# One decoder layer on Trainium2: projections whose PSUM bank is read once, and tasks that run before the weighted values

## The chip, the cores and the metric

The kernel runs on one core of a Trainium2 chip. A core has five engines with queues of their own: PE (matmul; its weight loads are listed as PEld), DVE (vector), ACT (scalar, activations), POOL and SP, which here only issues DMAs. Matmuls write to PSUM, which has eight banks of 128 partitions x 2 KB; DVE and ACT read it. An engine works its instructions in the order in which the program lists them and waits where an operand isn't ready. The metric is the device time in microseconds (us), the median over runs.

## The reference

A decoder layer on x of 4 x 1024 x 256 (batch, sequence, features), 16 heads of 16 features, everything in f32:

```python
x = x + self_attn(layernorm(x), w_qkv, w_out)             # windows of 128
x = x + cross_attn(layernorm(x), ctx, mask, Wq, bq, ...)  # 77 keys of context
x = x + ffn(layernorm(x), ...)                            # SwiGLU, int8 fake-quantised
```

Self-attention cuts the sequence into chunks of 128. The queries of a chunk see the keys of their own chunk, causally, and of the chunk before (the first chunk has none before). Scores are divided by sqrt(16), then softmax, then the weighted sum of the values, then `w_out`. Cross-attention has biases on q, k and v, 77 keys per batch entry, and a mask over these keys; in this data all rows of the mask are the same. The feed-forward part scales x, weights and hidden values to int8 steps and back. The change touches the two attention stages; of the rest only the queues of some transfers.

## The kernel before

**Heads and strips.** The 256 features are two halves (g). In a half, 128 features on 128 partitions are eight heads of 16 rows. They are handled as four strips (j) of 32 partitions; each strip holds an even and an odd head (o = 0, 1). A matmul on a strip contracts over its 32 rows. For head o the tile of the queries, `q[g, o]`, and of the keys, `k[g, o]`, therefore has the 16 rows of the *other* head emptied, and one of these spare rows does a service: in `k` it holds ones, and in `q` the negated maximum of each query's scores, so that the matmul of the weights yields score minus maximum. In cross-attention a second spare row of `q`, the next one, holds ones, and the keys' tile has the mask there; the first spare row is zero until the maximum arrives.

**Making q and k** (`project`, L344). 16 matmuls (L304) fill one bank, `ps_p`, with the projection of 512 columns (half a sequence, `hf`) for a half g. Then ACT reads the bank twice, once for each o, and multiplies by a column of ones and zeros per partition: L363 for queries in cross-attention (`qrows` carries the scale of the scores, the bias column the row of ones), L367 for queries and L369 for keys in self-attention. 48 projections run in the loop and its lead: 32 for self-attention, 16 for cross-attention.

**A unit of attention.** Work goes in units: of self-attention two query tiles for one (g, o), of cross-attention four, 96 in all, one *slot* each. Four steps belong to a unit or a group of units:

- `maxima` (L714): PE computes the scores of four strips into four banks `sc_n`, with queries on partitions (L725 for self-, L740 for cross-attention); DVE takes the maxima of each strip (L755: two instructions per strip with the causal mask; L766: one per strip).
- `put_maxima` (L774): once per (g, o) PE transposes the maxima (`ps_mx`, L777), ACT copies them to `mxT` (L781), and four DMAs on SP (L784) put them into the spare row of each strip of `q`.
- `weights` (L799): the scores again, keys on partitions, into four banks `sc_t` (L810, L839), whose order is that of the strips; ACT takes the exponential (L820, L842), and POOL zeroes what causality excludes (L824).
- `weighted_values` (L845): PE sums the values by the weights into one bank `ps_av` (L854, L864); DVE transposes it to `o_sb` (L878). `normalise` (L880) divides by the sum of the weights on DVE (`rec` L886, `aN` L888), and `by_features` (L895), for odd o only, transposes both heads' results to `aT` (L900).

**The order of the work** is written out by the loop at L1214. The maxima run five slots (`LEAD`) ahead of the weights. A slot does, in this order: the weighted values that are due, with normalise and by_features; *tasks* from a list with a cost, an earliest slot and a due slot (projections, `values`, the layer norm's transposes `ps_t`, `out_project` into `ps_op`, preparation of weights), up to 1.35 of cost; *asides* for DVE (layer-norm statistics at L192 and L194, quantising of weights at L598 to L608, up to 1.2); `put_maxima` where due; the maxima of a unit ahead; the weights of the present unit. The last slots (`tail`) have an order of their own. All these groups draw on one pool of eight banks that goes round: a group takes the oldest bank, and waits until its readers are done.

**Queues.** SP issues the loads, the maxima's transfers and most stores; ACT issues the last two stores at the end of the feed-forward part (L1522).

Of the kernel before, what the change touches and what calls it, by code (L numbers as in the profile page):

```python
# [18 lines left out]
P = 128  # L19
# [6 lines left out]
def decoder_layer(  # L26
# [175 lines left out]
    with ExitStack() as att:  # L202
# [14 lines left out]
        rows, qrows, onerow, nextrow = [], [], [], []  # L217
        for o in range(NS):
            m = wp.tile([P, 1], F32, name=f"rows{o}")
            w = wp.tile([P, 1], F32, name=f"onerow{o}")  # L220
            n2 = wp.tile([P, 1], F32, name=f"nextrow{o}")
            for dst, first, n in (
                (m, o * HD, HD),
                (w, (1 - o) * HD, 1),
                (n2, (1 - o) * HD + 1, 1),
            ):
                at = stage.tile([P, NJ, HD], F32, name="at", tag="at", bufs=4)
                nc.gpsimd.memset(at, 0.0)
                nc.gpsimd.affine_select(
                    out=at[:, :, 0:n],  # L230
                    in_=at[:, :, 0:n],
                    compare_op=ALU.not_equal,
                    fill=1.0,
                    base=-first,
                    pattern=[[-SL, NJ], [-1, n]],
                    channel_multiplier=1,
                )
                nc.vector.tensor_reduce(dst, at, AX.XY, ALU.max)
            q = wp.tile([P, 1], F32, name=f"qrows{o}")
            nc.vector.tensor_scalar(q, m, QSCALE, None, ALU.mult)  # L240
            rows.append(m)
            qrows.append(q)
            onerow.append(w)
            nextrow.append(n2)


        f = stage.tile([P, P], F32, name="cb_f", tag="stage")
# [96 lines left out]
        def project(job, g, which, hf):  # L344

            out = job.q if which == "q" else job.k
            w = job.wq if job.kind == "X" else (wq_s if which == "q" else wk_s)
            if hf == 0:
                for o in range(NS):
                    out[g, o] = next_of("qk", qks)  # L350
            ps = bank("ps_p")
            for c in range(NC):
                by_columns(
                    ps,
                    w[:, c, g * P : (g + 1) * P],
                    job.xnT[hf][:, c, :],
                    start=(c == 0),
                    stop=(c == NC - 1),
                )
            for o in range(NS):  # L360
                dst = out[g, o][:, hf * HS : (hf + 1) * HS]
                if job.kind == "X":
                    nc.scalar.activation(  # L363
                        dst, ps, AF.Identity, bias=job.bq[:, g, o : o + 1], scale=qrows[o]
                    )
                elif which == "q":
                    nc.scalar.activation(dst, ps, AF.Copy, scale=qrows[o])  # L367
                else:
                    nc.scalar.activation(dst, ps, AF.Identity, bias=onerow[o], scale=rows[o])  # L369
# [39 lines left out]
        begin.close()  # L409

        def attention(alike):
            turn.update(begun)
            arm = ExitStack()
# [14 lines left out]
            bq_p = wp.tile([P, NP, NS], F32, name="bq_p")  # L428
# [8 lines left out]
            def prep_cross():  # L437
# [4 lines left out]
                def load_biases():  # L442
                    with nc.allow_non_contiguous_dma(reason="256-element biases"):
                        for name, src in (("q", bq), ("k", bk)):
                            raws[name] = small.tile([P, NP], F32, name="raw_b")
                            nc.sync.dma_start(out=raws[name], in_=src.rearrange("(g p) -> p g", p=P))
                    nc.sync.dma_start(out=bv_b, in_=bv.partition_broadcast(SK))
                    nc.sync.dma_start(out=bo_b, in_=bo.partition_broadcast(P))

                def biases():  # L450
                    for name, dst, by, plus in (("q", bq_p, qrows, nextrow), ("k", bk_p, rows, onerow)):
                        for o in range(NS):
                            nc.vector.tensor_scalar(dst[:, :, o], raws[name], by[o], None, ALU.mult)
                            nc.vector.tensor_scalar(
                                dst[:, :, o], dst[:, :, o], plus[o], None, ALU.add
                            )

                def transposed(w, name, dst=None):
                    def load():
                        raws[name] = stage.tile([P, NC, D], F32, name="raw_w", tag="stage")  # L460
                        nc.sync.dma_start(out=raws[name], in_=w.rearrange("(c p) i -> p c i", p=P))
# [17 lines left out]
                def load_context():  # L479
                    raws["c"] = stage.tile([SK, B, D], F32, name="craw", tag="stage")  # L480
                    nc.sync.dma_start(out=raws["c"], in_=ctx_in.rearrange("b k d -> k b d"))
# [55 lines left out]
                def load_row():  # L537
                    raws["m"] = stage.tile([P, SK], I32, name="mrow", tag="stage")
                    nc.sync.dma_start(out=raws["m"], in_=mask[0, :].partition_broadcast(P))

                def add_row():
# [7 lines left out]
                    for o in range(NS):  # L549
                        for g in range(NP):  # L550
                            at = (1 - o) * HD + 1
                            nc.sync.dma_start(
# [4 lines left out]
                def load_mask():  # L557
                    raws["m"] = stage.tile([P, NT, SK], I32, name="mraw", tag="stage")
                    nc.sync.dma_start(out=raws["m"], in_=mask.rearrange("(t p) k -> p t k", p=P))
# [50 lines left out]
            def prep_ffn():  # L610


                def rows_of(w, dst, sc, f):
                    kept = {}

                    def load():
                        kept["raw"] = stage.tile([P, D], F32, name="raw_f", tag="stage")
                        if f < NF - 1:
                            nc.sync.dma_start(out=kept["raw"], in_=w[f * P : (f + 1) * P, :])
                        else:  # L620
                            for r in (0, HR):
                                nc.sync.dma_start(out=kept["raw"][r : r + HR], in_=w[f * P :, :])
# [18 lines left out]
                def down(c):  # L641
                    kept = {}

                    def load():
                        kept["raw"] = stage.tile([P, FF], F32, name="raw_d", tag="stage")
                        nc.sync.dma_start(out=kept["raw"], in_=w_down[c * P : (c + 1) * P, :])
# [127 lines left out]
            def put_maxima(job, g, o):  # L774
# [6 lines left out]
                nc.scalar.copy(mxT, ps[: NJ * NT, :P])  # L781
                for j in range(NJ):
                    row = j * SL + (1 - o) * HD
                    nc.sync.dma_start(  # L784
# [338 lines left out]
            for j, job in enumerate(jobs):  # L1123
# [59 lines left out]
                if S_:  # L1183
                    for t2 in range(NT // 2):
                        a, by = ((-3, -1) if j else (-1, -1), (-1, 1), (3, 3), (4, 4))[t2]
# [28 lines left out]
            for slot in range(first, last):  # L1214
# [21 lines left out]
                else:  # L1236
                    for args in values_of.get(slot, ()):
                        weighted_values(*args)
                        normalise(*args, tail)
                        if not tail:  # L1240
                            by_features(*args)
                spent = 0.0
                cap = 1.35 if now and ahead else 2.3
                while t := next_in(tasks, slot, spent, cap):
# [3 lines left out]
                    if fn is out_project:  # L1248
                        job, hf, t2 = args
                        if job.kind == "X" and t2 == HT // 2 - 1:  # L1250
                            third_norm(job.b, hf, slot)
                spent = 0.0
# [27 lines left out]
        def feed_forward():  # L1280
# [155 lines left out]
            for t0 in sorted(added_there):  # L1436
                nc.sync.dma_start(out=rows_out(t0), in_=xb[t0 // NT][:, t0 % NT : t0 % NT + 2, :])
# [59 lines left out]
            def down(q, t0, nt):  # L1497
                odd = t0 // HT % 2
                for t2 in range(nt // 2):
# [20 lines left out]
                    else:  # L1520
                        nc.vector.tensor_tensor(y, y, xb[b][:, t : t + 2, :], ALU.add)
                        (nc.scalar if t0 + 2 * t2 >= B * NT - 4 else nc.sync).dma_start(  # L1522
                            out=rows_out(t0 + 2 * t2), in_=y
                        )
# [70 lines left out]
```

## Time and profile before

| | us |
|---|---|
| median of 3 runs | 665.53 (665.24 to 666.23) |
| profiled execution, its own time | 663.93 |
| its span on the chip | 662.1 |
| PE busy, with waits inside a group | 613.3 (93%) |
| DVE busy | 542.7 (82%) |
| ACT busy | 367.6 (56%) |
| POOL busy | 268.8 (41%) |

The span is the time from the first to the last instruction; 1.8 us of the execution's own time lie around it. TensorE's granted clock was 0.99 of full speed. A row of the timeline gives the start, the time, the engine, the line and operation, the tile written and those read, and how many instructions it stands for; in brackets is the idle time before it and what ended that. Ends of matmuls are modelled, so the time of a group on PE is best read from its start to the start of the next. A row of the waits gives engine, line, the releaser, the sum of the waits, how often, and the longest. "who waited for it" counts the waits of other instructions that this line ended.

In 40 equal slices of the span, PE's and DVE's busy shares in tenths are these; the two attention stages fill about slices 2 to 32:

```profile
PE   9899999999999999999999999999999997787775
DVE  6878778868779799678997996897978787889896
```

### The profile page before, as it was taken

What the parts mean: (1) busy time and instruction counts of PE and PEld (TensorE: products, weight loads), DVE (VectorE), ACT (ScalarE), POOL (GpSimd) and SP (SyncE); (2) the same over time, 40 slices, a digit from 0 to 9 for tenths busy, and PEclk for the clock granted to TensorE, in tenths of its full rate; (3) what the DMA queues carried; (4) which work ended last, traced back from release to release, by engine and by line L of the source; (5) the groups of instructions that cost most, each with busy time, mean ns of one, the idle gap of its engine ahead of it and who ended that gap; (6) DMA issues with size and microseconds to landing.
All of it is one profiled execution on the core that took longest, in us unless ns stands there. A gap on an engine that the chain in (4) does not pass through costs nothing.

```text
span 662.1 us, 20220 instructions
## 1 busy us (share of the span) xinstructions
PE 613.3 (93%) x7857; PEld 350.9 (53%) x7862; DVE 542.7 (82%) x1922; ACT 367.6 (56%) x672; POOL 268.8 (41%) x520
## 2 busy tenths in 40 slices
PE   9899999999999999999999999999999997787775
PEld 6456566566555665654446666544443445333564
DVE  6878778868779799678997996897978787889896
ACT  2365564644555634645565366447556475788392
POOL 3164533647234667650044867526611141111032
PEclk9999999999999999999999999999999999989899
DMA  8100100000000000000000000000000020000057
GB/s 291 48 4 15 38 3 2 18 5 5 18 27 10 12 2 19 9 15 14 8 10 11 12 24 26 5 3 4 3 2 4 4 96 17 1 0 1 0 97 165
DMA packets 18080, 17.43 MB, mean 26 GB/s; under 512 B 2998, under 2 KB 17335, under 8 KB 17975
## 3 DMA queue, kind: packets, MB, share of 16 engines
q1 hardware_dynamic: 15239, 13.69, 6.4%
q0 software_dynamic: 1904, 1.84, 2.1%
q8 instruction: 64, 1.05, 0.7%
q10 hardware_dynamic: 832, 0.53, 0.3%
q14 instruction: 41, 0.34, 0.2%
HBM read 9.47 MB, written 6.03 MB: 23 GB/s over the span
## 4 chain that ended last, share of the span: by engine, by line
PE 61%; DVE 25%; ACT 7%; issue 5%; POOL 1%; DVEq 0%; ACTq 0%
PE ps_p L304 13%; PE ps_av L854 8%; PE sc_t L810 7%; PE sc_n L725 7%; PE ps_op L304 6%; PE ps_av L864 4%; PE sc_t L839 3%; DVE junk L755 3%; PE ps_v L304 3%; PE sc_n L740 3%; DVE bnst L192 2%; DVE o_sb L878 2%; ACT shared L369 2%; PE ps_idle L117 2%; DVE aT L900 2%
## 5 line engine op out<-in xcount | busy, mean ns | idle before, releaser
L755 DVE CUSTOM_DVE_ANT_0 junk<-sc_n,cboth 128x256 bf16<-128x256 f32 (+1 forms) x512 | 172.3, 402 | 35.1 <-PE sc_n L725 35.1
L820 ACT ACTIVATE pt<-sc_t 128x512 f32<-128x512 f32 (+1 forms) x256 | 125.4, 577 | 85.3 <-PE sc_t L810 85.3
L824 POOL TENSOR_SCALAR_AFFINE_SELECT pt<-pt 128x256 f32<-128x256 f32 x256 | 102.2, 407 | 116.1 <-ACT pt L820 105.5
L810 PE MATMUL sc_t<-shared 32*128 32x256 f32 (+1 forms) x1024 | 87.9, 377 | 1.4 <-DVE vx L530 0.3
L842 ACT ACTIVATE ptx<-sc_t 77x512 f32<-77x512 f32 x128 | 65.2, 596 | 37.0 <-PE sc_t L839 37.0
L725 PE MATMUL sc_n<-shared 32*128 32x256 f32 (+1 forms) x1024 | 73.6, 387 | 3.0 <-ACT shared L369 1.6
L810 PEld LDWEIGHTS sc_t<-shared 32*128 32x128 f32 x1024 | 65.5, 185 | 13.6 <-ACT shared L367 3.2
L320 POOL TENSOR_SCALAR xn<-x,mv,rs 128x256 f32<-128x256 f32 x56 | 69.6, 1249 | 0.0
L160 POOL TENSOR_SCALAR ve<-mv 128x4 f32<-128x4 f32 x20 | 4.6, 232 | 153.8 <-DVE mv L194 153.7
L878 DVE STREAM_TRANSPOSE o_sb<-ps_av 128x512 f32<-128x512 f32 x63 | 45.0, 714 | 24.4 <-PE ps_av L854 14.3
L304 PE MATMUL ps_p<-shared,w_s 128*32 128x512 f32 x512 | 60.9, 595 | 3.4 <-DVE mx L766 1.6
L725 PEld LDWEIGHTS sc_n<-shared 32*128 32x128 f32 x1024 | 45.7, 184 | 32.3 <-DVE mx L755 10.8
L854 PE MATMUL ps_av<-pt,vt 128*32 128x256 f32 (+1 forms) x1152 | 59.3, 349 | 3.0 <-DVE mx L755 2.6
L766 DVE TENSOR_REDUCE mx<-sc_n 128x4 f32<-128x308 f32 x128 | 51.8, 466 | 8.5 <-PE sc_n L740 8.3
L854 PEld LDWEIGHTS ps_av<-pt,vt 128*32 128x32 f32 x1152 | 34.9, 110 | 31.5 <-DVE mx L755 6.4
L839 PE MATMUL sc_t<-shared,kx 32*77 32x512 f32 x256 | 45.9, 599 | 0.0
L755 DVE DVE_READ_ACCUMULATOR2_ANT mx<- 128x1 f32 x512 | 42.4, 83 | 0.1
L864 PE MATMUL ps_av<-ptx,vx 77*32 77x512 f32 x256 | 35.9, 605 | 3.4 <-DVE mx L766 2.5
L363 ACT ACTIVATE shared<-ps_p,bq_p,qrows 128x512 f32<-128x512 f32 x32 | 23.1, 773 | 26.0 <-PE ps_p L304 26.0
L740 PEld LDWEIGHTS sc_n<-kx,shared 32*128 32x128 f32 x1024 | 31.7, 186 | 10.2 <-DVE rec L886 1.7
L740 PE MATMUL sc_n<-kx,shared 32*128 32x77 f32 x1024 | 36.5, 277 | 0.0
L1406 ACT ACTIVATE act<-pg,gsc 128x512 f32<-128x512 f32 x44 | 29.2, 687 | 11.4 <-PE pg L1391 6.3
(201 smaller groups left out, 984.8 us busy)
## 6 DMA issues: line engine op xcount, KB each, us to landing
x<-in_x_dram SPq DMA_DIRECT2D x8, 512.0 KB
shared<-mxT SPq DMA_DIRECT2D x128, 4.0 KB
out_dram<-x SPq DMA_DIRECT2D x7, 256.0 KB
out_dram<-shared POOLq DMA_DIRECT2D x7, 256.0 KB, 4.6
out_dram<-shared SPq DMA_DIRECT2D x7, 256.0 KB
w_s<-in_L_attn_w_qkv_dram SPq DMA_DIRECT2D x2, 384.0 KB
raw_d<-in_L_ffn_w_down_dram SPq DMA_DIRECT2D x2, 352.0 KB
raw_f<-in_L_ffn_w_gate_dram SPq DMA_DIRECT2D x5, 128.0 KB
```

The source lines that it names most:

```text
L304: nc.tensor.matmul(out[r], lhsT[:, r], rhs, skip_group_check=True, **on)
L320: eng.tensor_scalar(xn, xb[job.b][:, t, :], job.st[hf].mv[:, i, 0:1], job.st[hf].rs[:, i : i + 1], ALU.subtract, ALU.mult,)
L725: nc.tensor.matmul(banks[j][:, (i + 1) * 2 * P - n : (i + 1) * 2 * P], q[r, t * P : (t + 1) * P], k[r, k0 * P : k0 * P + n], start=True, s ...
L740: nc.tensor.matmul(banks[j][:, i * SK : (i + 1) * SK], q[r, t * P : (t + 1) * P], k[r, :], start=alike, stop=alike or i == HT - 1,)
L755: nc.vector.tensor_tensor_reduce(out=junk[:, 2 * P - n :], in0=banks[j][:, (i + 1) * 2 * P - n : (i + 1) * 2 * P], in1=cboth[:, 2 * P - n ...
L810: nc.tensor.matmul(banks[j][:, w : w + n], k[r, t * P : (t + 1) * P], q[r, t * P : t * P + n], start=True, stop=True,)
L820: nc.scalar.activation(pt.rearrange("p i a q -> p (i a q)")[:, :w], banks[j][:, :w], AF.Exp)
L824: nc.gpsimd.affine_select(out=pt[:, :, 0, :], in_=pt[:, :, 0, :], compare_op=ALU.is_ge, fill=0.0, base=0, pattern=[[0, 2], [1, P]], channe ...
L839: nc.tensor.matmul(banks[j][:SK], k[r, :], q[r, s], start=alike, stop=True)
L842: nc.scalar.activation(pt, banks[j][:SK], AF.Exp)
L854: nc.tensor.matmul(ps[j * SL : (j + 1) * SL, (a0 - t0) * P : (a1 - t0) * P], slot_of(job.vs[kb // 2][:, kb % 2], heads[j]), job.pts[g, o, ...
L864: nc.tensor.matmul(ps[j * SL : (j + 1) * SL, :], slot_of(vx[:, job.b], heads[j]), job.pts[g, o, j, hf], start=True, stop=True,)
```

## The change

It has four parts.

1. `project` reads `ps_p` once. The first ACT instruction takes the whole bank, both heads' rows, to one head's tile in SBUF (q: o = 1, k: o = 0, cross-attention: o = 1, with the bias and the scale); nothing is masked there. The second instruction copies that tile, from SBUF, to the other head's tile, with the column of ones and zeros as its scale. In the unmasked tile the other head's rows are harmless only where the other operand is zero, so which tile may stay unmasked is alternated between q and k.
2. The rows of ones (and, in cross-attention, of zeros) come by transfers from small constant tiles, `none_one` (rows of zeros or ones, filled by POOL at the start): in self-attention one transfer per (g, o), in `put_maxima`, ahead of those of the maxima, into the spare rows of `k`; in cross-attention two per projection, zeros into row 0 and ones into row 1 of each strip of `q[g, 1]`. That is 16 and 32 transfers, all on SP for this data. `qrows` and most of the small DVE work on biases go.
3. In the loop, tasks come ahead of the weighted values, normalise and by_features, except in the tail. The window of the second quarter of the values' projections starts one slot later, (0, 1) instead of (-1, 1).
4. Transfers go by a name, `queue_of[0]`: SP where the mask's rows are all the same, as here, ACT otherwise. With it the last two stores move from ACT's queue to SP's.

```diff
-            for o in range(NS):
-                dst = out[g, o][:, hf * HS : (hf + 1) * HS]
-                if job.kind == "X":
-                    nc.scalar.activation(
-                        dst, ps, AF.Identity, bias=job.bq[:, g, o : o + 1], scale=qrows[o]
+            half = [out[g, o][:, hf * HS : (hf + 1) * HS] for o in range(NS)]
+            if job.kind == "X":
+                nc.scalar.activation(
+                    half[1], ps, AF.Identity, bias=job.bq[:, g : g + 1], scale=QSCALE
+                )
+                nc.scalar.activation(
+                    half[0], half[1], AF.Identity, bias=nextrow[0], scale=rows[0]
+                )
+                for row in range(2):
+                    queue_of[0].dma_start(
+                        out=half[1][row : P : SL, :].rearrange("j (t q) -> j t q", q=P),
+                        in_=none_one[row].unsqueeze(1).to_broadcast([NJ, HT, P]),
                     )
-                elif which == "q":
-                    nc.scalar.activation(dst, ps, AF.Copy, scale=qrows[o])
-                else:
-                    nc.scalar.activation(dst, ps, AF.Identity, bias=onerow[o], scale=rows[o])
+                return
+            first = 1 if which == "q" else 0
+            nc.scalar.activation(half[first], ps, AF.Copy, scale=QSCALE if which == "q" else 1.0)
+            nc.scalar.activation(half[1 - first], half[first], AF.Copy, scale=rows[1 - first])
...
                 nc.scalar.copy(mxT, ps[: NJ * NT, :P])
+                if job.kind == "S":
+                    queue_of[0].dma_start(
+                        out=job.k[g, o][(1 - o) * HD : P : SL, :].rearrange(
+                            "j (t q) -> j t q", q=P
+                        ),
+                        in_=none_one[1].unsqueeze(1).to_broadcast([NJ, NT, P]),
+                    )
                 for j in range(NJ):
                     row = j * SL + (1 - o) * HD
-                    nc.sync.dma_start(
+                    queue_of[0].dma_start(
...
-                        a, by = ((-3, -1) if j else (-1, -1), (-1, 1), (3, 3), (4, 4))[t2]
+                        a, by = ((-3, -1) if j else (-1, -1), (0, 1), (3, 3), (4, 4))[t2]
...
-                else:
+                elif tail:
                     for args in values_of.get(slot, ()):
                         weighted_values(*args)
                         normalise(*args, tail)
-                        if not tail:
-                            by_features(*args)
                 spent = 0.0
                 cap = 1.35 if now and ahead else 2.3
                 while t := next_in(tasks, slot, spent, cap):
...
+                if not tail:
+                    for args in values_of.get(slot, ()):
+                        weighted_values(*args)
+                        normalise(*args, tail)
+                        by_features(*args)
                 spent = 0.0
                 while t := next_in(beside, slot, spent, 1.2):
...
-                        (nc.scalar if t0 + 2 * t2 >= B * NT - 4 else nc.sync).dma_start(
-                            out=rows_out(t0 + 2 * t2), in_=y
-                        )
+                        queue_of[0].dma_start(out=rows_out(t0 + 2 * t2), in_=y)
```

## The prediction

> **What bounds the kernel now.** I read five views of the one profiled execution, in this order: the busy times with the chain that ended last, the groups by line, who waited for the reads of the projections' bank, the timeline of some slots, and SP's waits. A change within 0.2% (1.3 us) is about what a measurement of this kernel cannot tell from none.
>
> ```profile
> PE 613.3 (93%) x7857; PEld 350.9 (53%) x7862; DVE 542.7 (82%) x1922; ACT 367.6 (56%) x672; POOL 268.8 (41%) x520
> PE 61%; DVE 25%; ACT 7%; issue 5%; POOL 1%; DVEq 0%; ACTq 0%
> L755 DVE CUSTOM_DVE_ANT_0 junk<-sc_n,cboth 128x256 bf16<-128x256 f32 (+1 forms) x512 | 172.3, 402 | 35.1 <-PE sc_n L725 35.1
> ```
>
> PE looks full, but its 93% holds waiting: a matmul group that waits for a bank of PSUM in its middle counts as busy. DVE carries 25% of the chain, so the loop between PE and DVE is as much of a bound as PE itself. ACT, with 56%, matters only where PE waits for one of its results. Next, who waited for ACT's three reads of ps_p:
>
> ```profile
> L363 ACT ACTIVATE shared<-ps_p,bq_p,qrows x32: 768/772/780, 256.4 to 500.7; 128x512 f32<-128x512 f32 x32
> ...
>   PEld sc_t L839: 3.1, 7
>   PEld sc_t L810: 2.5, 7
> ...
> L367 ACT ACTIVATE shared<-ps_p,qrows x32: 679/684/689, 14.1 to 345.7; 128x512 f32<-128x512 f32 x32
> ...
>   PEld sc_t L810: 3.2, 10
> ...
> L369 ACT ACTIVATE shared<-ps_p,onerow,rows x32: 767/774/779, 15.8 to 351.7; 128x512 f32<-128x512 f32 x32
> ...
>   PEld sc_t L810: 2.9, 6
> ```
>
> Weight loads of the weights' scores (sc_t) wait for the second of the two reads: its last bank is the one that the projection left. The timeline of a slot with weighted values and a projection (207.7 to 214.0; rows of other engines left out) shows the price and DVE's part:
>
> ```profile
> 206.17 1.61 PE L810 MATMUL sc_t<-shared 32*128 32x256 f32 x16
> 207.71 1.94 PE L854 MATMUL ps_av<-pt,vt 128*32 128x128 f32 x40
> 209.47 1.90 PE L304 MATMUL ps_p<-shared,w_s 128*32 128x512 f32 x16
> 211.29 1.15 PE L725 MATMUL sc_n<-shared 32*128 32x256 f32 x16
> 212.26 1.82 PE L810 MATMUL sc_t<-shared 32*128 32x256 f32 x16
> 214.01 1.92 PE L304 MATMUL ps_p<-shared,w_s 128*32 128x512 f32 x16
> ```
> ```profile
> 209.72 0.72 DVE L878 STREAM_TRANSPOSE o_sb<-ps_av 128x512 f32<-128x512 f32 x1 [0.51 <-PE ps_av L854]
> 210.47 0.25 DVE L886 RECIPROCAL rec<-o_sb 128x16 f32<-128x16 f32 x1
> 210.75 0.42 DVE L888 TENSOR_TENSOR aN<-o_sb,rec 128x256 f32<-128x256 f32 x1
> 211.21 0.71 DVE L900 STREAM_TRANSPOSE aT<-aN 128x512 f32<-128x512 f32 x1
> ...
> 212.53 0.41 DVE L755 CUSTOM_DVE_ANT_0 junk<-sc_n,cboth 128x256 bf16<-128x256 f32 x1
> ```
>
> From start to next start, the projection is 1.82 us, ps_av 1.76, sc_n 0.97, and sc_t 1.75; where nothing waits (192.83) sc_t takes 1.04. DVE does its chain (o_sb, rec, aN, on odd heads aT) while PE does the projection, then 0.68 us of asides, then the maxima. That cover is what the new order takes away.
>
> **Part 1: one read of the bank.** Removed: one of two reads of ps_p in 48 projections. The bank comes free some 0.7 us sooner (pair 1.45 us as in the row at 185.72, one alone at most 0.77). The slot at 185.55 needed it 1.17 us after the projection's end: two reads miss that, one read does not. In 15 slots with a projection and without weighted values (14 of self-attention, 1 of cross-attention) sc_t now lies 0.59 us over its free length on average: -8.8 us. In slots with weighted values I count the same gain with part 3. The waits shown sum to 11.7 us of weight loads; matmuls lose more, since the loads are refilled after the wait. So -8.8 is between 0 (if another wait ends last there) and -15 us.
>
> The second copy now waits on the first, on ACT's own queue; behind it stand mxT's copy and the exponentials. ACT's idle before the exponentials is 85.3 us on sc_t alone, so a few tenths there are covered; without cover 64 pairs x 0.1 us = 6 us at most. A source in SBUF costs no more by the rows: L939, two pointer operands, 256 columns, 514 ns; the PSUM reads with two pointers, 512 columns, 773 ns.
>
> [...]
>
> **Part 2: spare rows by transfers.** Added: 48 transfers on SP. Sixteen stand before the four of mxT in SP's queue:
>
> ```profile
> SPq L784 <- ACT mxT L781: 369.5, 32, 19.1
> ```
>
> SP idles there, and the new transfer waits only for PE's last use of k and for ACT, both a slot earlier, so it should be issued in that idle time: 0. Without that cover: one issue of 0.7 us (four take 2.80 at 202.16) delays the last row, which lands 3.54 us after the first issue with 0.47 us to spare: 16 x 0.23 = 3.7 us; at worst a landing (1.37 us) is added, 16 x 1.6 = 26 us. The 32 of cross-attention go ahead three slots early, 1.4 us of SP per projection, and cover is ample: 0, at most 16 x 0.2 = 3 us. The last two output transfers on SP instead of ACT: one more issue (0.7 us) at most behind another, 0; the two memsets on POOL and some seven small DVE instructions fewer lie in the start: 0 to -1 us.
>
> [...]
>
> **Part 3: tasks ahead of the weighted values.** In some 53 slots of attention both exist (30 self-, 23 cross-attention). New order: task (1.84 us), ps_av, sc_n, sc_t on PE; on DVE the chain can begin only when ps_av ends. During the task DVE finishes the maxima of the slot before and then idles, 1.5 us, which no other work fills: its queue holds o_sb next. The next slot's first group takes over the bank of sc_n's first strip (the pool of eight goes round, four sc_n and four sc_t to a slot), so PE waits until DVE has read it. From ps_av's end: 0.2 + chain 1.47 (2.21 with aT) + asides + first strip 0.75, against sc_n + sc_t = 2.01 us. That leaves 0.41 us (1.15 with aT) of waiting, plus the asides; in cross-attention, whose first strip takes 0.5 us and whose two groups 1.92, it is 0.24 (0.98).
>
> - By durations: 16 x 0.41 + 14 x 1.15 + 12 x 0.24 + 11 x 0.98 = 36.4 us, and 33 us of asides in these slots (0.6 to 1.2 us in 39 of them, counted to 1.0): 69 us.
> - By three slots of the trace that have this order already, because they have no task:
>
> ```profile
> 70.70 0.85 PE L810 MATMUL sc_t<-shared 32*128 32x256 f32 x16
> ...
> 71.36 0.71 DVE L900 STREAM_TRANSPOSE aT<-aN 128x512 f32<-128x512 f32 x1
> ...
> 72.66 1.92 PE L304 MATMUL ps_p<-shared,w_s 128*32 128x512 f32 x16 [1.11 <-DVE mx L755]
> ```
>
> Here sc_t takes 1.96 us instead of 0.89: 1.07 lost with aT and no asides. At 285.61, with 0.88 us of asides, PE waits till 288.10, 1.6 lost; at 507.60 in cross-attention 1.3 (mean 1.45 with both); at 503.73, with neither, 0. So 20 slots with aT and asides x 1.45, 5 with aT only x 1.07, 19 with asides only x 0.71 (1.45 less aT's 0.74), 9 with neither x 0.2: 50 us.
>
> From this comes off what the same 53 slots lose now, 25.7 us, their waits for the second read (14 us) among it. Part 3 costs +24 by stretches, +43 by durations; with part 1's -8.8, +15 or +35. I take +22, nearer the stretches, which are the order itself, though few. 663.9 (the execution's span 662.1 and 1.8 around it) + 22 = 686; the median of the runs stands 1.6 above that execution, so **687.5 us**.
>
> **Rivals.**
> - *The early bank wins (faster).* Speaks for it: the waits on L363 to L369, and 9 slots with neither aT nor asides. It decides below a mean wait of (25.7 + 8.8)/53 = 0.65 us in the 53 slots; at 0.4 us the sum is 21 - 34.5 = -13, 652 us; at 0.2, 642. Against it: three of the four slots above lose more than 1 us.
> - *The spare rows come late (slower).* Weights wait at sc_t for the fill or for mxT behind it, in 16 slots, from the point where the fill is issued after mxT's copy. Without part 3's loss: -8.8 + 3.7 to 26, 660 to 683, 672 with half of it. Against it SP's 369.5 us of idleness.
> - *Nothing moves (665.5).* Gain and loss are each hidden or meet: the waits at sc_t are replaced by equal ones.
>
> **How the numbers follow.** DVE's late chain 0.69, late spare rows 0.05, early bank 0.22, nothing 0.04. Likeliest: 687.5, its own range 679 (+15 less a little) to 704 (+35 and a late fill's 3.7). The range of 8 in 10 takes in most of the faster case: 650 to 704. Slower by over 0.2%: 0.69 + 0.05 = 0.74; within 0.04; faster 0.22.
>
> **What would show it.** Right: o_sb's idle time before it grows from 24 us by tens, DVE's busy time stays near 542 and its share falls below 80%; ps_av, ps_p or ps_op wait on mx at the start of slots; no weight load of sc_t waits for a read of ps_p; the projection slot without weighted values falls from 1.75 to 1.04 in sc_t. Wrong: sc_t's or the next first group's waits in the 53 slots below 0.65 us; or weight loads of sc_t that wait for a DMA (late rows); or ACT's mxT copies late behind the dependent copy. My sum is weakest in the asides, which stand in most of these slots and of which I have two examples.

## The result, and the profile after

The changed kernel takes 712.29 us (median of 4 runs, 706.83 to 713.43) against 665.75 us: 1.0675 times as long, 95% interval 1.0636 to 1.0715, or 46.5 us more. The forecast was slower, 687.5 us, with a range that ended at 704. The direction and the mechanism of the wait were right; the size was half of what came.

The profiled execution took 711.61 us, its span 709.9. From its page, the busy times, the chain's shares by engine and the row of `o_sb` (busy and mean ns, then the idle time before it and what ended that):

```profile
PE 606.7 (85%) x7862; PEld 340.8 (48%) x7862; DVE 542.0 (76%) x1915; ACT 369.0 (52%) x672; POOL 267.1 (38%) x522
PE 53%; DVE 35%; issue 6%; ACT 4%; POOL 1%; DVEq 0%; ACTq 0%
L895 DVE STREAM_TRANSPOSE o_sb<-ps_av 128x512 f32<-128x512 f32 x63 | 45.0, 715 | 80.5 <-PE ps_av L871 54.5
```

In the profile before, the row of `o_sb` is:

```profile
L878 DVE STREAM_TRANSPOSE o_sb<-ps_av 128x512 f32<-128x512 f32 x63 | 45.0, 714 | 24.4 <-PE ps_av L854 14.3
```

No engine has much more work than before: ACT's busy time grew by 1.4 us, DVE's 542 us are unchanged and PE's sum even fell by 7. The chain moved from PE to DVE (25% to 35%), and DVE's idle time before `o_sb` grew from 24.4 to 80.5 us. That is the idle time that the order was expected to open, some 1.1 us for each of the 53 slots where the forecast had put 1.5. The same piece of work as the one shown at 207.7 in the profile before (here with a `ps_v` task as well; rows of other engines left out) shows the rest of the loop, PE first, then DVE:

```profile
217.85 1.92 PE L871 MATMUL ps_av<-pt,vt 128*32 128x128 f32 x40
219.70 1.15 PE L735 MATMUL sc_n<-shared 32*128 32x256 f32 x16
220.67 1.09 PE L827 MATMUL sc_t<-shared 32*128 32x256 f32 x16
223.49 1.92 PE L306 MATMUL ps_p<-shared,w_s 128*32 128x512 f32 x16 [1.73 <-DVE mx L765]
```
```profile
219.86 0.72 DVE L895 STREAM_TRANSPOSE o_sb<-ps_av 128x512 f32<-128x512 f32 x1 [3.46 <-PE ps_av L871]
...
221.36 0.71 DVE L917 STREAM_TRANSPOSE aT<-aN 128x512 f32<-128x512 f32 x1
222.00 0.38 DVE L608 TENSOR_REDUCE wamax<-raw_f 128x1 f32<-128x256 f32 x1
...
222.68 0.41 DVE L765 CUSTOM_DVE_ANT_0 junk<-sc_n,cboth 128x256 bf16<-128x256 f32 x1
```

DVE stood idle for 3.46 us while PE did the tasks and `ps_av`. Then come its chain, 0.68 us of asides, and the maxima at 222.68. PE waits for the first strip until 223.49. The `sc_t` group itself no longer waits (1.09 us as the row has it); the wait is now behind it. The wait rows of the projections (engine, line, releaser: us in all, times, longest), two of before and then two of after, show the same over the whole run:

```profile
PE ps_p L304 <- DVE mx L766: 1.6, 1, 1.6
PE ps_p L304 <- DVE mx L755: 1.6, 3, 1.1
PE ps_p L306 <- DVE mx L765: 16.5, 15, 1.9
PE ps_p L306 <- DVE mx L776: 9.8, 10, 1.7
```

Adding the lengths of all `sc_t` groups, each from its start to the start of the next group on PE, gives 143.2 us before and 172.2 after: +29.0. All other groups of PE together grew by 19 us. The forecast had no term for those; the rows of the clock give part of it.

The profile's rows by stretches (columns: length, then busy time and count of PE, PEld, DVE, ACT and POOL, then TensorE's granted clock, DMA share and GB/s), around another such wait, that before the projection at 116.43:

```profile
113.08:116.49 3.41, 1.48 (x36) 1.25 (x40) 3.31 (x13) 1.83 (x5) 1.57 (x5) 1.00 0.02 4
116.49:119.90 3.41, 3.41 (x16) 0.55 (x16) 2.43 (x16) 0.00 (x0) 1.00 (x3) 0.50 0.28 78
119.90:123.32 3.42, 3.42 (x52) 2.00 (x52) 2.18 (x13) 2.57 (x5) 0.99 (x3) 1.00 0.02 5
```

In the first stretch PE is busy for 1.48 of 3.41 us; in the next, of the same length, the granted clock is 0.50, and the 16 matmuls of the projection take all of it. They take 1.8 us at full clock. In the attention stages there are nine such windows of half clock after the change, and there was one before (at 65.46). Two of the nine follow each other directly. At half speed each costs at most 3.41 / 2 = 1.7 us, the eight more 13.6 us.

### The profile page after: what moved, and what is told of

The parts are those of the page before. It is cut to its first block, busy times and chain, and to the rows that moved or that the text cites. A ratio compares the mean times of both kernels' runs of the same rounds, so it can differ in the third digit from the quotient of the medians.

```text
span 709.9 us, 20197 instructions
## 1 busy us (share of the span) xinstructions
PE 606.7 (85%) x7862; PEld 340.8 (48%) x7862; DVE 542.0 (76%) x1915; ACT 369.0 (52%) x672; POOL 267.1 (38%) x522
## 4 chain that ended last, share of the span: by engine, by line
PE 53%; DVE 35%; issue 6%; ACT 4%; POOL 1%; DVEq 0%; ACTq 0%
PE ps_p L306 14%; PE ps_av L871 8%; PE ps_op L306 7%; DVE o_sb L895 6%; PE sc_n L735 5%; DVE junk L765 4%; PE ps_v L306 4%; PE sc_t L827 3%; DVE aN L905 3%; PE ps_av L881 3%; DVE aT L917 3%; DVE bnst L192 3%; PE ps_t L337 2%; DVE mx L776 2%; DVE rec L903 2%
## 5 line engine op out<-in xcount | busy, mean ns | idle before, releaser
L895 DVE STREAM_TRANSPOSE o_sb<-ps_av 128x512 f32<-128x512 f32 x63 | 45.0, 715 | 80.5 <-PE ps_av L871 54.5
L306 PE MATMUL ps_p<-shared,w_s 128*32 128x512 f32 x512 | 65.5, 635 | 18.6 <-DVE mx L765 15.4
L735 PE MATMUL sc_n<-shared 32*128 32x256 f32 (+1 forms) x1024 | 77.2, 396 | 2.9 <-DVE mx L765 1.4
L827 PE MATMUL sc_t<-shared 32*128 32x256 f32 (+1 forms) x1024 | 71.5, 369 | 0.3 <-DVE kx L518 0.3
L735 PEld LDWEIGHTS sc_n<-shared 32*128 32x128 f32 x1024 | 47.8, 189 | 30.9 <-DVE mx L765 12.5
L827 PEld LDWEIGHTS sc_t<-shared 32*128 32x128 f32 x1024 | 58.5, 187 | 3.3 <-issue 0.8
L306 PE MATMUL ps_op<-wo_s,aT 128*32 128x256 f32 x512 | 33.7, 408 | 10.1 <-DVE mx L765 5.2
L377 ACT ACTIVATE shared<-ps_p 128x512 f32<-128x512 f32 x32 | 19.2, 600 | 42.2 <-PE ps_p L306 42.0
L306 PE MATMUL ps_p<-shared,wq_x 128*32 128x512 f32 x256 | 31.9, 617 | 8.7 <-DVE mx L776 6.9
L306 PEld LDWEIGHTS ps_p<-shared,w_s 128*32 128x32 f32 x512 | 14.4, 113 | 51.8 <-DVE mx L765 24.3
```

Of the source, the lines that this page charges most:

```text
L306: nc.tensor.matmul(out[r], lhsT[:, r], rhs, skip_group_check=True, **on)
L735: nc.tensor.matmul(banks[j][:, (i + 1) * 2 * P - n : (i + 1) * 2 * P], q[r, t * P : (t + 1) * P], k[r, k0 * P : k0 * P + n], start=True, s ...
L827: nc.tensor.matmul(banks[j][:, w : w + n], k[r, t * P : (t + 1) * P], q[r, t * P : t * P + n], start=True, stop=True,)
L895: nc.vector.transpose(job.av[g, o, hf], ps)
```

## The experiments

The kernels were compared with runs of the kernel before on the same chip; its median was 665.5 to 666.0 us each time.

### The old order with the rest of the change

```diff
-                elif tail:
+                else:
                     for args in values_of.get(slot, ()):
                         weighted_values(*args)
                         normalise(*args, tail)
+                        if not tail:
+                            by_features(*args)
...
-                if not tail:
-                    for args in values_of.get(slot, ()):
-                        weighted_values(*args)
-                        normalise(*args, tail)
-                        by_features(*args)
...
-                        a, by = ((-3, -1) if j else (-1, -1), (0, 1), (3, 3), (4, 4))[t2]
+                        a, by = ((-3, -1) if j else (-1, -1), (-1, 1), (3, 3), (4, 4))[t2]
```

> The changed kernel with the weighted values ahead of the tasks again (and the values' window back): one read of the bank and the transfers alone. Theory (the order carries the whole loss): the slots with a projection lose their wait for the second read, 8.8 us where there are no weighted values and up to 14 us where there are; some of it returns as a wait for DVE's maxima. 646 to 657 us, half-clock windows in attention as before (one), sc_t at 1.04 us in projection slots. Rival (the masked copy and the spare rows' transfers cost): 667 us or more.

663.11 us, ratio 0.9955 (0.9936 to 0.9974). The loss is gone, but only 2.4 us of gain is left where 9 to 20 were expected. Its waits name what took part of it, by the wait rows:

```profile
PEld sc_t L827 <- ACT mxT L791: 2.7, 6, 0.6
PEld sc_t L856 <- ACT mxT L791: 2.3, 4, 0.6
PE sc_t L827 <- DMA shared<-mxT: 2.0, 2, 1.3
```

None of these three is in the waits of the kernel before. The weights wait for the copy of the maxima on ACT, which stands behind the second head's copy, and in two places for the transfers of the maxima.

### The new order alone

The kernel before, with the loop of the change and the values' window (0, 1): on its lines, the diff above with plus and minus exchanged.

> The kernel before with only the order changed: tasks ahead of the weighted values, and the values' window. Theory: all of the loss and none of the single read's gain. In slots without weighted values the second read is waited for as before (some 7 us in the profile of the change), so 715 to 722 us, with six or more half-clock windows in attention. Rival (copies and transfers make much of the loss): under 700 us.

713.01 us, ratio 1.0709 (1.0679 to 1.0739). The order alone brings the whole loss: 47.5 us, and the rest of the change -2.4, together 45.1 against 46.5 measured. Its time is 2 us below the expected range, and its profile has five half-clock windows in attention where six or more were expected. What the single read and the transfers do to the new order nearly cancels: against this run, the changed kernel's `sc_t` groups take 6.4 us less (172.2 against 178.6), but its profile has four half-clock windows more. DVE's idle time before `o_sb` is 83.0 us here, 80.5 in the changed kernel.

### The transfers alone

The kernel before with both reads of the bank and, added to them, the 48 transfers, which write what the spare rows hold already; the last two stores go by SP.

```diff
+            if job.kind == "X":
+                dst = out[g, 1][:, hf * HS : (hf + 1) * HS]
+                for row in range(2):
+                    nc.sync.dma_start(
+                        out=dst[row : P : SL, :].rearrange("j (t q) -> j t q", q=P),
+                        in_=none_one[row].unsqueeze(1).to_broadcast([NJ, HT, P]),
+                    )
...
                 nc.scalar.copy(mxT, ps[: NJ * NT, :P])
+                if job.kind == "S":
+                    nc.sync.dma_start(
+                        out=job.k[g, o][(1 - o) * HD : P : SL, :].rearrange(
+                            "j (t q) -> j t q", q=P
+                        ),
+                        in_=none_one[1].unsqueeze(1).to_broadcast([NJ, NT, P]),
+                    )
...
-                        (nc.scalar if t0 + 2 * t2 >= B * NT - 4 else nc.sync).dma_start(
+                        nc.sync.dma_start(
```

> The kernel before with only the transfers: both reads of the bank stay, the 48 transfers write into the spare rows what stands there already, and the last two stores go by SP. Theory: SP's idle time covers them, 664.5 to 667.5 us. Rival (late rows): 4 to 26 us more, weights' loads of sc_t that wait for a transfer.

670.99 us, ratio 1.0086 (1.0059 to 1.0113): the rival's case, 5.5 us. The timeline of SP's queue in this run, then that of PE at the same place:

```profile
257.13 10.64 SPq L378 DMA_DIRECT2D shared<-fill  x4
267.87 0.39 SPq L631 DMA_DIRECT2D raw_f<-in_L_ffn_w_gate_dram  x1
268.35 0.56 SPq L795 DMA_DIRECT2D shared<-fill  x1
269.00 2.75 SPq L803 DMA_DIRECT2D shared<-mxT  x4
```
```profile
265.15 0.27 PE L789 MATMUL ps_mx<-ident,mx 128*32 128x128 f32 x1
...
269.49 1.13 PE L752 MATMUL sc_n<-kx,shared 32*128 32x77 f32 x32
271.63 0.66 PE L829 MATMUL sc_t<-shared 32*128 32x256 f32 x3 [1.02 <-DMA shared<-mxT]
```

The maxima of the last unit of a self-attention job were transposed at 265.15, but their transfers start at 269.00. Ahead of them in SP's queue stand cross-attention's transfers (L378), which wait for ACT's copy of the projection that was made in the same slot, then a load and the transfer of the ones. The weights wait for the maxima's rows. There are two such places, 2.4 us of waiting in all; behind the second lies a half-clock window (at 404.92), 1.7 us at most. The rest of the 5.5 us isn't traced.

### Self-attention's transfers without cross-attention's

The kernel of the run before, less the 32 transfers in `project`.

```diff
-            if job.kind == "X":
-                dst = out[g, 1][:, hf * HS : (hf + 1) * HS]
-                for row in range(2):
-                    nc.sync.dma_start(
...
```

> The kernel before with the 16 transfers of ones ahead of the maxima's in self-attention and the last two stores on SP, without cross-attention's 32. Theory (cross-attention's transfers, waiting for ACT's copy in front of the last puts of self-attention, cost the 5.5 us): 664.5 to 667 us. Rival (the transfer ahead of the maxima's delays the weights in 16 slots, or the stores cost): 669 to 672 us as with all of them.

664.99 us, ratio 0.9986 (0.9966 to 1.0006). So the 16 transfers ahead of the maxima's and the moved stores cost nothing that this can tell, and the 5.5 us come with cross-attention's 32. The forecast had feared the 16 and trusted the 32: it was the other way round.

### The old order, with the second head's copy put off

```diff
-                nc.scalar.activation(
-                    half[0], half[1], AF.Identity, bias=nextrow[0], scale=rows[0]
-                )
-                for row in range(2):
...
+                def second():
+                    nc.scalar.activation(
+                        half[0], half[1], AF.Identity, bias=nextrow[0], scale=rows[0]
+                    )
+                    for row in range(2):
...
+                deferred.append(second)
                 return
...
-            nc.scalar.activation(half[1 - first], half[first], AF.Copy, scale=rows[1 - first])
+            deferred.append(
+                lambda: nc.scalar.activation(
+                    half[1 - first], half[first], AF.Copy, scale=rows[1 - first]
+                )
+            )
...
                 for args in puts.get(slot, ()):
                     put_maxima(*args)
+                while deferred:
+                    deferred.pop(0)()
```

The bank is read at once, as in the change. The copy within SBUF and cross-attention's transfers come after the slot's maxima have been put.

> The old order with one read of the bank, and the second head's copy (with cross-attention's two transfers behind it) put off until the slot's maxima have been put. It is to remove the two waits that took the gain of the run with the old order: weight loads of sc_t on mxT's copy, which stood behind the copy on ACT (5.0 us, 10 times), and the two last puts of self-attention, whose transfers stood behind cross-attention's on SP (2 us, with up to two half-clock windows of 1.7 us). Theory: 663.1 less 5 to 10 = 653 to 658 us, no sc_t wait on mxT's copy, no wait for a transfer of mxT. Rival (the bank's early release is worth no more than 2 us, and another wait ends last): 660 to 664 us.

650.33 us, ratio 0.9761 (0.973 to 0.9792): 15.6 us faster than the kernel before, more than expected, and the best version here. The three waits above are gone from its rows. From its page, the busy times and the chain; from its groups by line, the row of `o_sb`:

```profile
PE 595.4 (92%) x7862; PEld 342.3 (53%) x7862; DVE 541.8 (84%) x1915; ACT 365.0 (56%) x672; POOL 269.0 (42%) x522
PE 56%; DVE 31%; issue 6%; ACT 5%; POOL 1%; DVEq 0%; ACTq 0%
L907 DVE STREAM_TRANSPOSE o_sb<-ps_av 128x512 f32<-128x512 f32 x63 | 45.0, 714 | 14.7 <-PE ps_av L883 8.0 <-PE ps_av L893 4.6 <-POOL aN L917 1.2
```

PE's busy time is 17.9 us below that of the kernel before for the same matmuls: those were mostly waits inside groups. (Its profile has no half-clock window in attention, that of the kernel before has one, 1.7 us at most.) All `sc_t` groups together take 124.9 us, 18.3 less than before. So the single read of the bank is worth most of what the waits on it promised, once the copy behind it is out of the way.

### Only cross-attention's transfers put off

The old order with the rest of the change, and:

```diff
-                for row in range(2):
-                    queue_of[0].dma_start(
...
+                def fills():
+                    for row in range(2):
+                        queue_of[0].dma_start(
...
+                deferred.append(fills)
                 return
...
                 for args in puts.get(slot, ()):
                     put_maxima(*args)
+                while deferred:
+                    deferred.pop(0)()
```

> The run with the old order (663.1 us), with cross-attention's transfers alone put off until the slot's maxima have been put; the second head's copy stays where it is. Theory (the transfers in front of the last puts cost 5.5 us, the copy in front of mxT's copy the rest of the 12.8 us that putting off both gave): 656 to 660 us, sc_t's wait on mxT's copy still near 5 us. Rival (the copy is the whole of it): 662 to 664 us; or (the transfers are the whole): 650 to 652 us.

656.96 us, ratio 0.9867 (0.9837 to 0.9898): 6.1 us less than with the old order, and its wait on `mxT`'s copy is still there (2.7 and 2.3 us in the same two rows). Putting off the copy as well gives the other 6.6, of which up to 3.4 may be the clock: this run's profile has two half-clock windows in attention, that of the best version none. The waits shown were 5.0 us for the copy and 2.0 for the transfers, smaller than what their removal brought. For the transfers the rows of the clock hold part of the reason: the run with the old order has half clock right after each of the two waits, at 268.98 and 398.68, and this run has none at these places, but one at 280.93. That is three windows in attention against two, so one window, 1.7 us at most; what makes up the rest isn't shown.

### The new order with the asides after the maxima

```diff
-                spent = 0.0
-                while t := next_in(beside, slot, spent, 1.2):
-                    spent += t[3]
-                    t[4](*t[5])
...
                     maxima(*ahead)
+                spent = 0.0
+                while t := next_in(beside, slot, spent, 1.2):
+                    spent += t[3]
+                    t[4](*t[5])
```

> The changed kernel with DVE's asides after the maxima instead of ahead of them. Theory: the wait at the next slot's first bank is lag + chain + asides + first strip less sc_n and sc_t; without the asides 0.4 (1.15 with aT) in self-attention and 0.25 (1.0) in cross-attention remain, 36 us in 53 slots against 59 measured: -22 us, and as the long idle stretches of PE vanish most of the eight extra half-clock windows (1.7 us each, 14 us) go too: 676 to 690 us. Rival (asides are not what delays the maxima, or they return as a later wait): 705 to 713 us with the windows unchanged.

679.86 us, ratio 1.0213 (1.0179 to 1.0247): 32 us less than the changed kernel by moving some small DVE instructions past the maxima. Two half-clock windows are left in attention, and the `sc_t` groups take some 3 us more than in the kernel before, where the change had 29 more. So in this order the asides between the end of `ps_av` and the first strip of the maxima are paid by PE, as the sum for the wait had it. The chain alone is still paid: against the 124.9 us of the best version, `sc_t` here takes some 21 more.

### The old order, copy put off, asides after the maxima

The best version with the edit just shown.

> As the run before it (old order, one read, copy put off), and DVE's asides after the slot's maxima. In the old order the waits at a slot's first bank are some 9 to 12 us in all, most of them in slots with asides. Theory: they come earlier by the asides' time: 3 to 8 us less than the run before it. Rival (the asides then delay the next slot's o_sb chain, and the maxima behind it): the same or more.

653.7 us, ratio 0.9821 (0.9785 to 0.9857), against 0.9761 without the move: 3.4 us slower rather than 3 to 8 faster. The rival's time came, but its reason isn't shown. PE's own waits for `mx` did get shorter (6.4 us in all against 15.6); against that, this profile has two half-clock windows in attention, that of the best version none, and at 1.7 us each they could be the whole difference.

### Work in PE's waits, to hold the clock

The changed kernel, with the matmuls of `sc_t` issued twice in some slots, the same values into the same banks. The repeats do nothing but fill PE's wait.

```diff
-                    w = 0
-                    for i in range(2):
+                    for _ in range(again):
+                        w = 0
+                        for i in range(2):
...
-                    for j in range(NJ):
+                    for j in range(NJ * (again if alike else 1)):
+                        j = j % NJ
...
-                    weights(*now)
+                    odd = not tail and any(args[2] for args in values_of.get(slot, ()))
+                    weights(*now, again=2 if odd else 1)
```

In the first run the slots are those in which the values of an odd head are due; in the second, where a list of slots takes the place of `odd`, the 20 slots after which PE waited at least 1.3 us.

> The changed kernel (new order), with the 16 (8) matmuls of sc_t issued twice, the same values into the same banks, in slots where the weighted values of an odd head are due: some 27 slots, whose first bank after sc_t came 1 to 2.4 us late. The repeats fill PE's wait and add about 1 us of PE work to each of these slots. Theory (a wait of PE brings half-clock windows, 1.7 us each, eight more than before): the repeats are hidden in the wait, two to four windows are left in attention, and the time falls by 5 to 12 us: 700 to 707. Rival (the windows do not come from the waits, or cost nothing since PE waits for DVE anyway): 711 us or more, and up to 27 us more where the repeats are not hidden.

> The changed kernel with sc_t's matmuls issued twice in the 20 slots alone after which PE waited 1.3 us or more in the profile of the change (the repeats take about 1 us, so all of it should lie in the wait). Theory (a wait within the clock's 3.4 us window brings the half clock, 1.7 us each): at most three half-clock windows in attention instead of nine, 8 to 12 us less than the change: 700 to 704 us. Rival (the windows cost nothing on the path): 711 to 714 us.

The first: 709.07 us, ratio 1.0632 (1.0602 to 1.0663), with three half-clock windows in attention. That many were expected, but the time fell by only 3.2 us, less than expected, and the intervals overlap, so it may be nothing. In part of the slots the wait seems to have been shorter than the repeats: cross-attention's `sc_t` groups took 3.7 us more in all. The second: 704.85 us, ratio 1.0595 (1.0537 to 1.0653), again with three windows; the forecast for it ended at 704. Here the kernel with useless work is 7.4 us faster by the medians; the intervals of its ratio and the change's overlap a little (its upper end 1.0653, the change's lower 1.0636). Its own runs spread with the clock, 702.07 us at a mean of 0.987 and 709.20 at 0.978. Its timeline at the place of the stretches shown above:

```profile
116.75 1.49 PE L828 MATMUL sc_t<-shared 32*128 32x256 f32 x32
119.52 1.92 PE L306 MATMUL ps_p<-shared,w_s 128*32 128x512 f32 x16 [1.28 <-DVE mx L765]
121.37 0.93 PE L735 MATMUL sc_n<-shared 32*128 32x256 f32 x12
```

The wait that is left is 1.28 us, and the projection takes 1.85 us to the next group instead of 3.55. If the whole difference is the clock's, six windows fewer for 7.4 us are some 1.2 us each, and the eight more of the change come to about 10 us. That is an estimate from two profiles and two medians whose intervals overlap a little. The run with the new order alone fits it: four windows fewer than the changed kernel, 6.4 us more in `sc_t`, and nearly the same time.

## Why the prediction was wrong

**Part 3 (the order), right in mechanism.** The steps came as stated: DVE idle during the tasks, the chain late, the maxima behind it, PE waiting at the next slot's first bank. The order alone carries the loss.

**The step that failed: a sum that counts one wait of PE and nothing else.** "Part 3 costs +24 by stretches, +43 by durations; with part 1's -8.8, +15 or +35. I take +22": all of this is the wait at and behind `sc_t`; what becomes of PE's other groups is put at nothing, without a reason. Of the 47.8 us by which the profiled span grew, the `sc_t` groups hold 29.0, the other groups of PE 19.

**The larger miss: the clock and other groups.** No step asked what PE's longer waits do to TensorE's granted clock. The half-clock windows went from one to nine, about 10 us by the estimate from the repeats, 13.6 at most. Where they lie fits that: `ps_p`, `ps_op` and `sc_n` hold 23.5 us of half clock after the change and none before, and grew by 9.0 us together. A little of the `sc_t` groups' 29 us is half clock too (5.0 us of it after the change, 1.9 before). Waits and clock give 665.75 + 29 + 10 = 705 of the 712. Of the 7 to 8 us left, the groups of `ps_av` make 5.3. There the clock isn't the reason (1.6 us of half clock after, 1.5 before). They grew by 4.4 us in the run with the new order alone as well, so this goes with the order; how it comes about stays open.

**The smaller miss: the size of the wait.** Net +22 was taken, nearer the stretches ("the order itself, though few"), and the `sc_t` groups, behind which the wait lies, measured +29.0. Neither sum was the right one: in the slots with a task and weighted values, `sc_t` came out 59 us over its free length (the figure in the expectation of the run with the asides later), about halfway between the 50 of the stretches and the 69 of the durations.

**Part 1 (one read), right, and a little smaller than the sum.** The read alone releases the bank in time: in the changed kernel no weight load of `sc_t` waits for a read of `ps_p`. The forecast's -8.8 for slots without weighted values and 14 for the others made 22.8; with the old order and the copy put off 18.3 us of `sc_t` and 15.6 of time came. But "a few tenths there are covered" failed: the second copy delays `mxT`'s copy on ACT, and in the old order putting it off brought 6.6 us. No row gives the 0.1 us a pair that was set for a wait of the second copy on the first: it was the author's estimate, and after the change ACT idles 1.0 us in all ahead of 32 of the copies and 0.5 us ahead of the other 16, some 0.03 us each. "A source in SBUF costs no more by the rows" did not hold either: a copy takes 722 ns from SBUF and 684 from PSUM, 38 ns more (41 in cross-attention, last section), and there are 48 such copies, not 64, so 1.9 us of ACT's time in all.

**Part 2 (transfers), wrong about which.** "Cover is ample: 0" for cross-attention's 32 was the failing step: their own rows are early, but they wait for ACT's copy in front of another job's maxima on SP, 5.5 us in the kernel before. In the changed kernel this costs nothing that shows: no row has PE waiting for a transfer of `mxT`. Perhaps its longer slots leave enough time; no run shows that. The 16 of self-attention and the two stores cost 0, as said.

**The rival of the early bank** (faster) did not come, but its gain was real: it was outweighed by the order in the change, and in the old order mostly hidden by the queues of ACT and SP.

**Signs.** "o_sb's idle time grows by tens", "DVE's share falls below 80%", "no load of sc_t waits for a read of ps_p" and "first groups wait on mx" all held, and in the slot at 213.36, with a projection and without weighted values, `sc_t` took 1.03 us to the next group.

## What to carry to other kernels

An instruction order for one engine is also an order for its consumers: before moving independent work ahead of a producer, ask what covered the producer's chain on the other engine, and count everything that stands in that engine's queue between the producer's end and the next release of a buffer. Here the order alone cost 47.5 us, and moving the asides past the maxima took 32 us off the changed kernel. When a result is made earlier by splitting an instruction in two, put only the half that releases the buffer early; the other half belongs behind whatever waits for that engine's queue, and so does any transfer that waits for it: 663.11 us with both at once, 650.33 us with both put off. When waits of a busy PE grow, look at its granted clock and add a term for it: here the one half-clock window in attention became nine, some 10 us by the estimate. And ask of a sum for one group what it leaves at nothing for the others.

## What the runs showed of the hardware

Most half-clock windows of the changed kernel came behind waits shorter than a window. In the 3.41 us ahead of six of its nine windows in attention begins an idle stretch of PE of 1.7 to 2.4 us, ahead of a seventh (at 31.16) one of 2.9; with repeats in such waits three windows were left. The starts of five of the nine (31.16, 116.49, 259.85, 304.22, 406.62 us) lie apart by whole multiples of 3.413 us (25, 42, 13 and 30), and each lasts 3.41. So in this execution they sit on a grid of 3.413 us, and what can be compared is how busy PE was in the grid's interval ahead. Rows of three such intervals, and for the second and the third also the one that follows:

```profile
208.65:212.06 3.41, 1.53 (x18) 0.42 (x16) 3.41 (x20) 1.64 (x4) 1.56 (x4) 1.00 0.14 43
403.21:406.62 3.41, 1.42 (x32) 0.96 (x28) 3.31 (x16) 1.64 (x4) 3.15 (x6) 1.00 0.02 5
406.62:410.04 3.42, 3.42 (x38) 1.71 (x30) 2.02 (x10) 0.00 (x0) 2.49 (x3) 0.50 0.14 41
451.00:454.41 3.41, 1.90 (x49) 1.62 (x48) 3.27 (x6) 1.73 (x6) 2.81 (x4) 1.00 0.04 11
454.41:457.82 3.41, 2.55 (x24) 1.19 (x28) 1.94 (x6) 0.20 (x1) 3.41 (x6) 0.50 0.03 6
```

With 1.42 and 1.48 us of PE's busy time the clock fell; with 1.53 it stayed once, and with 1.90 it fell once. Over all intervals of the changed kernel's attention stages, the clock fell behind each of the five with 1.50 us or less, and behind two of the nine with 1.53 to 1.90. The other two windows follow an interval with 2.41 us of busy time and one with 3.38, itself at half clock. So these rows show no sharp bound in the profile's busy time, and none in the waits: behind the wait of 1.67 us that ended at 304.17 came a window, behind that of 1.73 us that ended at 223.49 none. One reason may lie in the busy time itself. The one window in attention of the kernel before, at 65.46, follows stretches in which PE counts as busy almost throughout:

```profile
62.00:63.00 1.00, 0.62 (x2) 0.29 (x2) 1.00 (x7) 1.00 (x3) 0.93 (x1) 1.00 0.00 0
63.00:64.00 1.00, 1.00 (x4) 0.54 (x4) 1.00 (x9) 0.74 (x2) 1.00 (x4) 1.00 0.00 0
64.00:65.00 1.00, 1.00 (x13) 0.58 (x15) 0.96 (x7) 0.00 (x0) 0.92 (x4) 1.00 0.00 0
```

In the first two there are only some six matmuls. They belong to a group of `sc_n` whose 16 matmuls take 0.97 us in the row at 211.29 and more than 2.5 us here: it waits inside the group, and the profile counts that as busy.

The runs of the changed kernel spread with the clock: 706.83 us at a mean clock of 0.978, and 711.61 to 713.43 at 0.969 to 0.972.

The two forms of ACT's read also measured: from PSUM without a pointer operand 598 ns, the masked copy within SBUF with one 722, for 128x512. With one pointer operand from PSUM it was 684 before, so the source in SBUF costs 38 ns. In cross-attention, with two pointer operands, it was 772 ns from PSUM before and 813 from SBUF after, 41 ns more.
